# Windowed layer's channel products on quarters of TensorE, stores from ScalarE's queue, and a new order of steps in an eight-part decoder kernel

## The chip, the cores and the metric

The kernel runs on one core of one Trainium2 chip. The metric is device microseconds of one execution. The kernel before takes 1657.0 us (median of 3 runs, 1656.43 to 1660.24).

## The reference

A residual stream `x` of 16 x 64 rows of 512 floats passes four pairs of attention and feed-forward, each added to the stream after a layer norm, all in fp32 but where bf16 is named:

```python
x = x + L0_xattn(norm(x), ctx)   # windowed attention over 16 positions, 64 channels, 8 heads
x = x + L0_ffn(norm(x))          # int8-quantised gate/up/down
x = x + L1_xattn(norm(x), ctx)   # 32 query heads, 8 key heads of 128, q and k RMS-normed
x = x + L1_ffn(norm(x))          # block-scaled 4-bit weights and activations (bf16 products)
x = x + L2_xattn(norm(x), ctx)   # 32 heads of 16
x = x + L2_ffn(norm(x))          # router, 16 of 64 low-rank experts
x = x + L3_xattn(norm(x), ctx)   # 16 query heads, 4 key heads of 96
x = x + L3_ffn(norm(x))          # 3-bit weights, dequantised

def L0_xattn(x, cond, Wq, bq, Wk, bk, Wv, bv, Wo, bo):   # x as (16, 64 channels, 512)
    q, k, v = (W @ src + b for ...)                      # W is 64 x 64, over the channels
    dots = sum over a head's 8 channels of q[t] * k[t + w], w in 16 window places
    out = softmax(dots * 8 ** -0.5) applied to v[t + w]
    return Wo @ out + bo
```

## The kernel before

The stream lies in SBUF as 8 tiles of 128 rows (two of the 64-row sequences each). Two lanes of work are written into one program and one instruction order. The **main** lane (lane `a`, four PSUM banks) does `normed_attention` (the second layer's attention) on all tiles, then the rest of the layers on tiles 4 to 7. The **side** lane (lane `b`, four other banks) does the first layers (`WindowAttention`, then `Int8Ffn`) for groups of two tiles, then the later layers on tiles 0 to 3. `merged` runs the main generator and, after each step, advances the side generator by as much estimated cost as the main step yielded, times a rate. A `Need` makes the main lane stop until the side lane has reached a mark, so that a group's first layers are in the stream before the main lane reads it; meanwhile only side work is written. TensorE's order is that of the writing. The other engines' orders are made by a scheduler; `behind_main` puts an instruction behind the main lane's latest VectorE instruction.

`normed_attention` has two loops over `ticks`, which runs every step of a unit with a lag in ticks. The first, the **context stage**, has 32 units: keys and values of the context (`ps_ckv`, L757), a copy `ckv` (L766), squares (L768), a factor `r` by GpSimd's power (L123), scaled keys turned by TensorE (`ps_ckT`) and written back (L782), and a store `saved` to DRAM (L784) from SyncE's queue. The buffer of `ckv` is used again six units on. The second, the **main loop**, has 64 units; a tick writes `scores`, `scale`, `queries` (`ps_q`), `project` (`ps_wo`, added to the stream by VectorE at L157), `turn` (`ps_qT`, `ps_kT`), `keys_values` (`ps_kv`), `turn_weights` (`ps_pT`), `values` (`ps_a`), in this order. Each of the eight takes a PSUM bank, and four banks go round, so each result waits for the reader of the fourth before it.

`WindowAttention` multiplies two sequences of 64 channels at a time with a block-diagonal 128 x 128 weight `wbd`: for each tile three products to `qs`, `kp`, `vp` (`inputs`, L323) and one, in two halves of the columns, for the output (`project`, L461). `dots` are products on VectorE summed over channels by TensorE on 32-column tiles of the array (L364). They go through DRAM to another layout (`dots_d`, L374 and L376), through a softmax on VectorE, ScalarE and GpSimd (`softmax`), through DRAM again (`att_d`, L400), and are loaded spread over 8 channels each (`att`, L412; four buffers). `output` then forms products (L438) and sums (L448, GpSimd) over 8 window groups. The first group yields an extra pause of 16 before `output`, and 4 after it.

All DMAs stand in SyncE's queue. Some waits there are for a buffer to come free and some for an earlier transfer on the same completion counter.

`small_head_attention` holds products on tiles of the array of 32 rows by 64 columns (L1101). `mxfp4_ffn` takes ticks of quantise 8.0, product 0.9, turn 0.3.

Of the kernel before, what the change touches and what calls it, by code (L numbers as in the profile page):

```python
# [8 lines left out]
F32 = mybir.dt.float32  # L9
# [219 lines left out]
class WindowAttention:  # L229
# [4 lines left out]

    WIN, LEFT, NH = 16, 8, 16
# [4 lines left out]
    def __init__(self, es, ln, ctx_in, wt, bias):  # L240
        self.ln, self.ctx_in = ln, ctx_in
        k, nc = ln.k, ln.nc
        NH = self.NH
        pool = ln.pool(es, "l0c", 1)

        self.group = pool.tile([P, 2, 2 * NH], F32, tag="group", name="group")
        nc.gpsimd.memset(self.group, 0.0)
        for j in range(2):
            nc.vector.tensor_reduce(
                self.group[:, j, NH * j : NH * (j + 1)],  # L250
                k.ident.rearrange("p (h d) -> p h d", d=8),
                AX.X,
                ALU.add,
            )
        self.dram = es.enter_context(
            ln.tc.tile_pool(name="turned", bufs=2, space=bass.MemoryType.DRAM)
        )

        self.wbd = pool.tile([P, 4, P], F32, tag="wbd", name="wbd")
        nc.gpsimd.memset(self.wbd, 0.0)  # L260
        self.bcol = pool.tile([P, 4], F32, tag="bcol", name="bcol")
        for r in range(2):
            rows = slice(r * S, (r + 1) * S)
            nc.sync.dma_start(self.wbd[rows, :, rows], wt)
        nc.sync.dma_start(self.bcol, bias)

    def run(self, tiles, pause=0.0):

        self.pause = pause
        with ExitStack() as es:  # L270
            self.pool = self.ln.pool(es, "l0a", 1)
            cns = [self.context(t) for t in tiles]
            yield 0.0
            xns = [self.normed(t) for t in tiles]
            yield 5.0
            kept = []
            for xn, cn in zip(xns, cns):
                kept.append(self.inputs(xn, cn))
                yield 3.0
            scores = []  # L280
            for qs, kp, _ in kept:
                dots = yield from self.dots(qs, kp)
                scores.append(dots)
            weights = []
            self.loads = []
            for n, dots in enumerate(scores):
                kept_weights = yield from self.softmax(dots)
                weights.append(kept_weights)
                if n == 0:
                    self.source = weights  # L290
                    for _ in range(3):
                        self.load()
            yield 2.0 + self.pause
            rest = None
            for i, t in enumerate(tiles):
                rest = yield from self.output(i, t, kept[i][2], rest)
            yield 4.0 + self.pause / 4
            rest()
# [11 lines left out]
    def inputs(self, xn, cn):  # L310

        ln, nc, pool, LEFT = self.ln, self.ln.nc, self.pool, self.LEFT
        qs = pool.tile([P, D], F32, tag="qs", name="qs", bufs=2)
        kp = pool.tile([P, D + self.WIN], F32, tag="kp", name="kp", bufs=2)
        vp = pool.tile([P, D + self.WIN], F32, tag="vp", name="vp", bufs=2)
        for pad in (kp, vp):
            nc.gpsimd.memset(pad[:, :LEFT], 0.0)
            nc.gpsimd.memset(pad[:, LEFT + D :], 0.0)
        for j, (src, dst) in enumerate(
            ((xn, qs), (cn, kp[:, LEFT : LEFT + D]), (cn, vp[:, LEFT : LEFT + D]))  # L320
        ):
            ps = ln.bank([P, D], "ps_qkv")
            nc.tensor.matmul(ps, lhsT=self.wbd[:, j, :], rhs=src, start=True, stop=True)  # L323
            nc.scalar.activation(dst, ps, AF.Identity, bias=self.bcol[:, j : j + 1])
        return qs, kp, vp
# [5 lines left out]
    def dots(self, qs, kp):  # L331
# [23 lines left out]
        for n, (b, j) in enumerate(steps):  # L355
            prods = ahead
            if n + 1 < len(steps):
                ahead = products(*steps[n + 1])
            if n == 0:
                yield 1.0  # L360
            if j == 0:
                ps = ln.bank([P, D], "ps_dot")
            for w in range(NB // 2):
                nc.tensor.matmul(  # L364
                    ps[32 * w : 32 * (w + 1)],
                    lhsT=self.group[:, j, :],
                    rhs=prods[w // 2][:, w % 2, :],
                    start=j == 0,
                    stop=j == 1,
                )  # L370
            yield 2.5 if n else 1.5
            if j == 1:
                nc.scalar.copy(dots[:, b, :], ps)
                nc.sync.dma_start(dram[b], dots[:, b, :])  # L374
# [6 lines left out]
    def softmax(self, e):  # L381


        ln, nc = self.ln, self.ln.nc
        WIN, NPC, L = self.WIN, self.NPC, self.L
        n_at_once = L // 2
        for c in range(2):
            part = e[:, :, c * n_at_once : (c + 1) * n_at_once]
            by_place = part.rearrange("p w n -> p n w")
            mx = ln.small.tile([P, n_at_once], F32, tag="mx0", name="mx0")  # L390
            nc.vector.tensor_reduce(mx, by_place, AX.X, ALU.max)
            nc.vector.tensor_tensor(part, part, bc(mx, 1, WIN), ALU.subtract)
            nc.scalar.activation(part, part, AF.Exp, scale=8.0**-0.5)
            sm = ln.small.tile([P, n_at_once], F32, tag="sm0", name="sm0")
            nc.vector.tensor_reduce(sm, by_place, AX.X, ALU.add)
            nc.vector.reciprocal(sm, sm)
            nc.gpsimd.tensor_tensor(part, part, bc(sm, 1, WIN), ALU.mult)
            yield 3.0
        dram = self.dram.tile([WIN // 2, self.NH, 2 * D], F32, tag="att", name="att_d")
        nc.sync.dma_start(  # L400
            dram.rearrange("g h (q m) -> (h q) g m", q=NPC),
            e.rearrange("p (g w) n -> p g (w n)", w=2),
        )
        return dram
# [12 lines left out]
    def output(self, i, t, vp, rest):  # L417

# [13 lines left out]
        for g in range(n_groups):  # L432
# [22 lines left out]
            if g == 3 and rest is not None:  # L455
                rest()

        def project():
            po = ln.bank([P, D], "ps_o")
            for w in range(2):  # L460
                nc.tensor.matmul(  # L461
                    po.rearrange("p (a q n) -> p a q n", a=2, n=L),
                    lhsT=self.wbd[:, 3, :],
                    rhs=acc[:, :, :, w, :],
                    start=w == 0,
                    stop=w == 1,
                )
            x = ln.k.x[t]
            nc.vector.scalar_tensor_tensor(x, po, self.bcol[:, 3:4], x, ALU.add, ALU.add)

        return project
# [204 lines left out]
def normed_attention(ln, groups, rates, w_in, w_kv, norms):  # L676
# [7 lines left out]
    with ExitStack() as es:  # L684
# [59 lines left out]
        def factors(r, sq):  # L744

            nc.vector.tensor_reduce(r, sq, AX.X, ALU.add)
            nc.vector.tensor_scalar(r, r, 1.0 / HD, 1e-6, ALU.mult, ALU.add)  # L747
            ln.rsqrt(r, r)

        def context_keys(u):  # L750
# [18 lines left out]
            r = ln.small.tile([P, 5], F32, tag="r", name="r")[:, 0:2]  # L769
            factors(r, sq)  # L770
# [8 lines left out]
        def context_turn(u):  # L779
# [4 lines left out]
            nc.sync.dma_start(saved[u], both)  # L784
# [33 lines left out]
        def keys_values(u):  # L818
# [19 lines left out]
            factors(r, sq)  # L838
# [39 lines left out]
        def project(u):  # L878
# [9 lines left out]
            [(4, context_turn, 0.3), (2, context_scale, 0.0), (0, context_keys, 3.4)],  # L888
# [6 lines left out]
                (1, scale, 0.0),  # L895
                (0, queries, 3.4),
                (5, project, 3.4),
                (1, turn, 0.7),
                (0, keys_values, 1.7),
                (3, turn_weights, 0.4),  # L900
                (4, values, 0.9),
# [5 lines left out]
def mxfp4_ffn(ln, tiles, w_in, bias, kept_w):  # L907
# [10 lines left out]
    with ExitStack() as es:  # L918
# [76 lines left out]
        yield from ticks(units, [(0, quantise, 8.0), (2, product, 0.9), (1, turn, 0.3)])  # L995
# [181 lines left out]
def lora_experts(ln, tiles, w_a, w_r, w_b):  # L1177
# [13 lines left out]
    with ExitStack() as es:  # L1191
        pool = ln.pool(es, "l2f")
        wr = pool.tile([P, NC, KE], F32, tag="wr", name="wr", bufs=1)
        nc.sync.dma_start(wr.rearrange("p c n -> p (c n)"), w_r)
# [359 lines left out]
def decoder_kernel(ctx: ExitStack, tc: tile.TileContext, i: dict, out: bass.AP):  # L1554
# [8 lines left out]

    def first_layers(ln):
        with ExitStack() as es:
# [13 lines left out]
            first = attention.run(groups[0], 16.0)  # L1579
# [9 lines left out]
            for _ in range(6):  # L1589
                yield next(first)  # L1590
            yield MARK
            ffn.load()
            for t in range(2, NT):
                load(t)
            for n, tiles in enumerate(groups):
                yield from first if n == 0 else attention.run(tiles)
                yield from ffn.run(tiles)
                yield MARK

    def last_layers(ln, tiles):  # L1600
        yield from small_head_attention(ln, tiles, i["l2a_w"])
        yield from lora_experts(ln, tiles, i["l2f_a"], i["l2f_r"], i["l2f_b"])
# [4 lines left out]
    def side():  # L1607
        yield from first_layers(b)
        b.pages(ctx)
        yield from mxfp4_ffn(b, halves[0], i["l1f_w"], i["l1f_b"], kept_w)  # L1610
# [20 lines left out]
def laid_out(a):  # L1631
# [10 lines left out]
    i["l0a_w"] = np.stack([a[f"L0_xattn_W{n}"].T for n in "qkvo"], 1)  # L1642
# [72 lines left out]
```

## Time and profile before

The profiled execution took 1651.44 us, its span from first to last instruction 1649.7 us at a granted clock of 0.995; the runs' median is 1657.0 us.

| engine | busy us | share of the span | instructions |
|---|---|---|---|
| TensorE (PE) | 1596.5 | 97% | 7020 |
| its weight loads (PEld) | 929.2 | 56% | 7024 |
| VectorE (DVE) | 962.3 | 58% | 1998 |
| ScalarE (ACT) | 619.3 | 38% | 1929 |
| GpSimd (POOL) | 508.2 | 31% | 524 |

By stage, in us of busy time:

| stage, us from the start | length | PE | DVE | ACT | POOL | granted clock |
|---|---|---|---|---|---|---|
| start, 0 to 17 | 17 | 10.71 | 9.60 | 5.72 | 2.72 | 1.00 |
| context, 17 to 158 | 141 | 139.83 | 99.88 | 48.21 | 71.96 | 1.00 |
| hand-over, 158 to 182 | 24 | 12.39 | 12.54 | 3.75 | 8.00 | 0.77 |
| main loop with side work, 182 to 1115 | 933 | 913.93 | 610.77 | 386.57 | 345.64 | 0.99 to 1.00 |
| later layers, 1115 to 1650 | 535 | 519.66 | 229.51 | 175.03 | 79.90 | 1.00 |

An fp32 product is recorded as two passes of the array, so counts of matmuls are twice those of the code; transposes are one pass. A pass is recorded longer than the distance to the next, since passes overlap: busy time is not work done at the array's peak.

### The profile page before, as it was taken

Reading aid. Unit: us, or ns where it says so; the run is one execution under the profiler, and the core shown is the slowest. Engines: PE = TensorE matmul, PEld = TensorE weight load, DVE = VectorE, ACT = ScalarE, POOL = GpSimd, SP = SyncE. Lnnn points to the kernel's source line nnn. Section 1 sums busy time; section 2 is a strip of 40 time slices with the busy share of each in tenths; the row PEclk is TensorE's granted clock in tenths of the full one; section 3 lists DMA queues with packets and bytes.
Section 4 is the critical chain, followed back from the end, with each engine's and each line's share of the span. In section 5 each row is a group of like instructions: output and inputs, shape, how many; then the busy total and the mean of one; then the engine's idle time right before and its main releaser. Section 6 shows DMA issues by size and latency. Waiting matters only on the chain.

```text
span 1649.7 us, 20730 instructions
## 1 busy us (share of the span) xinstructions
PE 1596.5 (97%) x7020; PEld 929.2 (56%) x7024; DVE 962.3 (58%) x1998; ACT 619.3 (38%) x1929; POOL 508.2 (31%) x524
## 2 busy tenths in 40 slices
PE   8999799999999999999999999999999999999999
PEld 2334356664566645666565565554566566456774
DVE  6596498757776576766964465337345343422335
ACT  3333354344433344334343354221235432223442
POOL 1294237632484214843221232101012110011112
PEclk9999899999999999999999999999999999999999
DMA  8893159524882337934532321122120101201120
GB/s 272 248 290 113 44 155 281 169 87 139 235 257 77 129 120 211 252 133 150 183 128 96 122 80 69 54 109 85 59 71 20 48 20 51 90 16 58 39 71 26
DMA packets 98872, 200.32 MB, mean 121 GB/s; under 512 B 49488, under 2 KB 66768, under 8 KB 86992
## 3 DMA queue, kind: packets, MB, share of 16 engines
q1 hardware_dynamic: 98768, 199.00, 38.8%
q8 instruction: 57, 0.93, 0.2%
q14 instruction: 47, 0.39, 0.1%
HBM read 179.57 MB, written 19.40 MB: 121 GB/s over the span
## 4 chain that ended last, share of the span: by engine, by line
PE 87%; DVE 5%; DMA 3%; ACT 2%; POOL 1%; issue 1%; SPq 0%; ACTq 0%; POOLq 0%; DVEq 0%
PE ps_wo L670 16%; PE ps_q L805 11%; PE ps_ckv L757 6%; PE ps_kv L823 6%; PE ps_q L1411 5%; PE ps_s L620 5%; PE ps_a L661 5%; PE ps_o L1262 3%; PE ps_pT L141 3%; PE ps_h L1237 3%; PE ps_v L1358 3%; PE ps_k L1395 3%; PE ps_dot L364 2%; PE ps_q L1083 2%; PE ps_wo L1151 2%; PE ps_o L1324 2%
## 5 line engine op out<-in xcount | busy, mean ns | idle before, releaser
L670 PE MATMUL ps_wo<-l1a_o,aT 128*128 128x512 f32 x512 | 231.5, 595 | 2.0 <-ACT aT L875 2.0
L805 PE MATMUL ps_q<-l1a_w,kvT 128*128 128x512 f32 x512 | 231.8, 596 | 0.0
L645 POOL TENSOR_TENSOR p<-p,sm 128x512 f32<-128x512 f32 x96 | 103.1, 1074 | 362.2 <-DVE sm L644 328.3
L636 ACT ACTIVATE p<-ps_s,mx 128x128 f32<-128x128 f32 x384 | 135.6, 370 | 162.0 <-DVE mx L631 143.5
L123 POOL TENSOR_TENSOR r<-r,mhalf 128x5 f32<-128x5 f32 (+1 forms) x96 | 101.0, 1052 | 304.5 <-DVE r L747 284.7
L157 DVE TENSOR_TENSOR x<-x,ps_wo 128x512 f32<-128x512 f32 x104 | 71.2, 685 | 199.3 <-PE ps_wo L670 171.6
L670 PEld LDWEIGHTS ps_wo<-l1a_o,aT 128*128 128x128 f32 x512 | 95.4, 190 | 118.4 <-issue 111.1
L805 PEld LDWEIGHTS ps_q<-l1a_w,kvT 128*128 128x128 f32 x512 | 93.3, 192 | 95.9 <-issue 95.8
L448 POOL TENSOR_TENSOR acc<-acc,pv 128x512 f32<-128x512 f32 x96 | 126.3, 1339 | 7.5 <-DVE pv L438 6.4
L823 PE MATMUL ps_kv<-l1a_w,kvT 128*128 128x256 f32 x512 | 121.4, 380 | 0.6 <-ACT qn L815 0.6
L757 PE MATMUL ps_ckv<-l1a_kv,kvT 128*64 128x512 f32 x512 | 116.9, 598 | 0.5 <-ACT ckv L766 0.5
L823 PEld LDWEIGHTS ps_kv<-l1a_w,kvT 128*128 128x128 f32 x512 | 92.6, 190 | 14.3 <-issue 1.9
L123 POOL TENSOR_TENSOR rs<-rs,mhalf 128x1 f32<-128x1 f32 x64 | 36.8, 580 | 206.7 <-DVE rs L132 195.0
L620 PEld LDWEIGHTS ps_s<-kT,qT 128*128 128x128 f32 (+1 forms) x704 | 89.8, 193 | 6.2 <-issue 2.1
L620 PE MATMUL ps_s<-kT,qT 128*128 128x128 f32 (+1 forms) x704 | 91.9, 276 | 0.0
L343 DVE TENSOR_TENSOR prod<-qs,kp 128x1024 f32<-128x1024 f32 x64 | 77.5, 1248 | 14.5 <-PE ps_dot L364 7.6
L670 PE MATMUL ps_wo<-l3a_o,aP 128*128 128x512 f32 x192 | 85.6, 593 | 0.0
L1411 PE MATMUL ps_q<-kvT,l3a_w 128*128 128x256 f32 x384 | 85.5, 379 | 0.0
L652 DVE COPY pT<-ps_pT 128x512 f32<-128x512 f32 x96 | 64.2, 682 | 35.1 <-PE ps_pT L141 35.1
L438 DVE TENSOR_TENSOR pv<-att,ps_v 128x512 f32<-128x512 f32 x128 | 81.0, 676 | 3.5 <-DMA att<-att_d 3.3
L853 ACT COPY qT<-ps_qT 128x512 f32<-128x512 f32 x64 | 37.5, 587 | 120.7 <-PE ps_qT L141 120.7
L141 PE MATMUL ps_pT<-ident,p 128*128 128x128 f32 x512 | 72.8, 274 | 8.1 <-DVE x L157 8.1
(194 smaller groups left out, 2725.8 us busy)
## 6 DMA issues: line engine op xcount, KB each, us to landing
l1a_w<-in_l1a_w SPq DMA_DIRECT2D x32, 1536.0 KB, 6.9
att<-att_d SPq DMA_DIRECT2D x64, 512.0 KB, 7.8
l1a_o<-in_l1a_w SPq DMA_DIRECT2D x32, 1024.0 KB, 5.1
s<-ckv SPq DMA_DIRECT2D x32, 256.0 KB, 5.9
l3a_w<-in_l3a_w SPq DMA_DIRECT2D x6, 1024.0 KB, 5.5
l3a_o<-in_l3a_w SPq DMA_DIRECT2D x8, 768.0 KB, 4.1
l1a_kv<-in_l1a_kv SPq DMA_DIRECT2D x4, 1024.0 KB, 7.9
dots_d<-dots SPq DMA_DIRECT2D x16, 256.0 KB, 2.9
```

Source lines behind the costliest of these rows:

```text
L123: self.nc.gpsimd.tensor_tensor(out, v, self.k.mhalf[:, : v.shape[1]], ALU.pow)
L141: self.nc.tensor.transpose(ps[:, c, :], src[:, c * P : (c + 1) * P], ident)
L448: nc.gpsimd.tensor_tensor(sums, before, pv, ALU.add)
L620: nc.tensor.matmul(ps[:, i, :], lhsT=qT[:, i // 2, 2 * (i % 2) : 2 * (i % 2) + 2, :].rearrange("p g s -> p (g s)"), rhs=kTs[i // 2], start ...
L636: nc.scalar.activation(p[:, i, :], ps[:, i, :], AF.Exp, bias=mx[:, i : i + 1], scale=self.scale, accum_out=sm[:, i : i + 1],)
L645: nc.gpsimd.tensor_tensor(p, p, bc(sm, 2, P), ALU.mult)
L661: self.nc.tensor.matmul(ps[:, j, :, :], lhsT=v[:, j, :], rhs=pT[:, j, :], start=True, stop=True)
L670: self.nc.tensor.matmul(ps, lhsT=a, rhs=wo[:, g, :], start=g == 0, stop=g == len(chunks) - 1)
L757: nc.tensor.matmul(ps[j * S : (j + 1) * S], lhsT=k.context(c, 2 * t + 1 - j), rhs=w_pair[hp][:, c, :], start=c == 0, stop=c == NC - 1,)
L805: nc.tensor.matmul(ps, lhsT=k.stream(c, t), rhs=w_qkv[n][0][:, c, :], start=c == 0, stop=c == NC - 1,)
L823: nc.tensor.matmul(ps, lhsT=k.stream(c, t), rhs=w_qkv[n][1][:, c, :], start=c == 0, stop=c == NC - 1,)
L1411: nc.tensor.matmul(ps[:, j], lhsT=wq[:, c, (j0 + j) * P : (j0 + j + 1) * P], rhs=k.kvT[:, c, t : t + 2, 1:3, :], start=c == 0, stop=c == N ...
```

## The change

- `wbd` (block-diagonal) becomes `w4`, one DMA of a weight laid out in all four 64 x 64 quarters. `at_once` does a pair of products as four matmuls of 64 rows by 64 columns, one on each quarter. `inputs` becomes `keys_values` for each tile and one `queries` for both; `project` does both tiles of a group after the second `output`, where the first tile's stood within the second's.
- In the first group, `dots_d` and `att_d` are stored from ScalarE's queue; in all groups `saved` is. The int8 weights are asked for behind the first group's dots and tiles 2 to 7 of `x` behind its attention, as the program writes it; the pause of 16 becomes 2. In the other groups the softmax's VectorE steps stand behind the main lane's.
- Context stage: the factors of two units are computed together, and scaling and turning lag 3 and 5 ticks (2 and 4 before).
- Main loop: `project` stands ahead of `queries`, `values` ahead of `turn_weights`.
- `mxfp4_ffn`: quantise 6.5 and turn 1.8 of the tick's 9.2. The router's weights of `lora_experts` are loaded once for both lanes.

```diff
-        for r in range(2):
-            rows = slice(r * S, (r + 1) * S)
-            nc.sync.dma_start(self.wbd[rows, :, rows], wt)
+        nc.sync.dma_start(self.w4, wt)
...
+        self.pause, self.first = pause, late is not None
+        self.queue = self.ln.nc.scalar if self.first else self.ln.nc.sync
...
-            for xn, cn in zip(xns, cns):
-                kept.append(self.inputs(xn, cn))
-                yield 3.0
+            for n, cn in enumerate(cns):
+                keys.append(self.keys_values(n, cn))
+                yield 1.5
+            queries = self.queries(xns)
+            yield 3.0
...
+            if late is not None:
+                late()
...
+    def at_once(self, *products, start=True, stop=True):
+        for r in range(2):
+            rows = slice(r * S, (r + 1) * S)
+            for ps, j, src, swapped in products:
+                out = slice((r ^ swapped) * S, ((r ^ swapped) + 1) * S)
+                self.ln.nc.tensor.matmul(
+                    ps[out], lhsT=self.w4[rows, j, out], rhs=src[rows], start=start, stop=stop
+                )
+    def keys_values(self, n, cn):
...
+        pss = [ln.bank([P, D], "ps_kv0") for _ in range(2)]
+        self.at_once((pss[0], 1, cn, n), (pss[1], 2, cn, 1 - n))
...
+    def queries(self, xns):
...
+        self.at_once(*[(ps, 0, xn, n) for n, (ps, xn) in enumerate(zip(pss, xns))])
...
-                nc.sync.dma_start(dram[b], dots[:, b, :])
+                self.queue.dma_start(dram[b], dots[:, b, :])
...
-            nc.vector.tensor_reduce(mx, by_place, AX.X, ALU.max)
-            nc.vector.tensor_tensor(part, part, bc(mx, 1, WIN), ALU.subtract)
+            with ExitStack() if self.first else ln.behind_main():
+                nc.vector.tensor_reduce(mx, by_place, AX.X, ALU.max)
+                nc.vector.tensor_tensor(part, part, bc(mx, 1, WIN), ALU.subtract)
...
-            if g == 3 and rest is not None:
-                rest()
...
+    def project(self, tiles, accs):
...
+        for w in range(2):
+            self.at_once(
+                *[
+                    (po, 3, acc[:, :, :, w, :], 1 - n)
+                    for n, (po, acc) in enumerate(zip(pos, accs))
+                ],
+                start=w == 0,
+                stop=w == 1,
+            )
...
+            if n % 2 == 0:
+                fresh.append(ln.small.tile([P, 5], F32, tag="r", name="r"))
+            r = fresh[-1][:, 2 * (n % 2) : 2 * (n % 2) + 2]
+            nc.vector.tensor_reduce(r, sq, AX.X, ALU.add)
+            if n % 2:
+                factors(fresh[-1][:, 0:4])
...
-            nc.sync.dma_start(saved[u], both)
+            nc.scalar.dma_start(saved[u], both)
...
-            [(4, context_turn, 0.3), (2, context_scale, 0.0), (0, context_keys, 3.4)],
+            [(5, context_turn, 0.3), (3, context_scale, 0.0), (0, context_keys, 3.4)],
...
+                (5, project, 3.4),
                 (0, queries, 3.4),
-                (5, project, 3.4),
                 (1, turn, 0.7),
                 (0, keys_values, 1.7),
+                (4, values, 0.9),
                 (3, turn_weights, 0.4),
-                (4, values, 0.9),
...
-        yield from ticks(units, [(0, quantise, 8.0), (2, product, 0.9), (1, turn, 0.3)])
+        yield from ticks(units, [(0, quantise, 6.5), (2, product, 0.9), (1, turn, 1.8)])
...
-            first = attention.run(groups[0], 16.0)
+            first = attention.run(groups[0], 2.0, ffn.load)
```

## The prediction

> **What bounds the kernel.** I read the page's first part, the groups by shape on PE, PE's waits, and the timelines of the places they name.
>
> ```profile
> PE 1596.5 (97%) x7020; PEld 929.2 (56%) x7024; DVE 962.3 (58%) x1998; ACT 619.3 (38%) x1929; POOL 508.2 (31%) x524
> ```
>
> No other engine passes 58%, so what counts is PE's work and PE's waits. The groups by shape (busy, mean of one | idle before) give the work:
>
> ```profile
> L323 PE MATMUL ps_qkv<-cn,wbd 128*128 128x512 f32 x32 | 16.3, 634 | 0.0
> ...
> L461 PE MATMUL ps_o<-acc,wbd 128*128 128x512 f32 x32 | 15.2, 599 | 0.0
> ...
> L757 PE MATMUL ps_ckv<-l1a_kv,kvT 128*64 128x512 f32 x512 | 116.9, 598 | 0.5 <-ACT ckv L766 0.5
> ...
> L1101 PE MATMUL ps_s<-kbd,qT 32*64 32x128 f32 x512 | 10.4, 279 | 0.8 <-DVE x L157 0.8
> ```
>
> Busy over count is what a pass costs among its neighbours. A full-array pass costs 0.475 us at L461, a half-array one (128*64) 0.228 at L757: two share the array. At L1101 it is 10.4/512 = 0.020 for 128 columns, where a full pass of 128 columns costs about 0.11 (below): most of eight small tiles run together.
>
> PE's timeline (start, length, idle before) gives the step without overlap:
>
> ```profile
> 508.71 3.60 PE L670 MATMUL ps_wo<-l1a_o,aT 128*128 128x512 f32 x8
> 512.15 0.60 PE L141 MATMUL ps_qT<-ident,qn 128*128 128x128 f32 x4
> 512.58 0.27 PE L141 MATMUL ps_kT<-ident,kn 128*128 128x128 f32 x1
> ```
>
> Eight passes take 512.15 - 508.71 = 3.44, 0.43 each; a transpose (512.58 - 512.15)/4 = 0.11.
>
> PE's waits (total, times, longest):
>
> ```profile
> PE ps_pT L141 <- DVE x L157: 8.1, 4, 3.2
> ...
> PE ps_o L989 <- ACT xT L979: 3.6, 5, 0.8
> ...
> PE ps_wo L670 <- ACT aT L875: 2.0, 3, 0.7
> ...
> PE ps_a L661 <- DVE x L157: 1.8, 2, 1.1
> ```
>
> The other large ones lie in the hand-over, where the side lane alone is written. PE's timeline there:
>
> ```profile
> 159.94 0.41 PE L141 MATMUL ps_ckT<-ident,ckn 128*128 128x128 f32 x2 [1.50 <-DVE ckn L776]
> ...
> 165.07 1.98 PE L583 MATMUL ps_dn<-w_l0f,qT 128*128 128x512 f32 x4 [1.05 <-POOL qT L534]
> 170.23 0.44 PE L141 MATMUL ps_q<-ident,xs 128*128 128x128 f32 x2 [3.17 <-DVE xs L526]
> 171.98 3.78 PE L583 MATMUL ps_dn<-w_l0f,qT 128*128 128x512 f32 x4 [1.31 <-POOL qT L534]
> 175.56 1.06 PE L141 MATMUL ps_xT<-ident,xn 128*128 128x128 f32 x4
> 181.20 1.11 PE L141 MATMUL ps_xT<-ident,xn 128*128 128x128 f32 x4 [4.59 <-DVE rs L132]
> 182.11 4.91 PE L805 MATMUL ps_q<-l1a_w,kvT 128*128 128x512 f32 x8
> ```
>
> Last, VectorE's timeline at the longest L157 wait:
>
> ```profile
> 634.97 1.98 DVE L391 TENSOR_REDUCE mx<-dots 128x32 f32<-128x512 f32 x2 [4.52 <-DMA dots<-dots_d]
> ...
> 639.18 0.68 DVE L157 TENSOR_TENSOR x<-x,ps_wo 128x512 f32<-128x512 f32 x1
> ```
>
> VectorE stood at the side lane's softmax, waiting for a DMA, and the main lane's add stood behind it with a PSUM bank.
>
> **Quarter products.** A group has 2 x 3 + 2 x 2 = 10 full products, 20 passes, 8.6 us. After, it has 20 products of half the size on each side, in five sets of four, 40 passes. With all four quarters at once a set costs two steps, 0.86, a group 4.3. The trace shows no 64*64 tile. Bounds: no overlap, 40 x 0.43 = 17.2; full overlap, 4.3. I take 4.3, as L1101 is the nearest row. Entering and leaving a tiled shape costs: a context tick (64.65 to 68.60 in the timeline, 3.95) holds 16 half passes (3.44) and two transposes (0.22), so 0.3. Three visits a group: 0.9. Saved per group: 8.6 - 4.3 - 0.9 = 3.4; for groups 1 to 3, where PE is full, 10.2 us.
>
> In the first group the three products stand at the start, where the end is set elsewhere: `prod` began at 10.90 after `kp` and now waits for `qs`, ScalarE's fifth 0.69 us step. Context rows land about 1 us earlier (one issue fewer, smaller queue ahead), PE begins near 5.6 on the half clock (0.85 a pass), has three sets done at 10.5, ScalarE reaches `qs` at 11.4. So first `ps_ckv` at 17.1 against 16.57: +0.5. The first group's output saves 1.7 - 0.3 = 1.4.
>
> A rule that speaks against this part is the Trainium skill's "TensorEngine Tiling (Array Packing)", Restrictions and Gotchas: different row tiles cannot access one PSUM bank at the same time. At L1101 the row groups write different banks, so this trace does not test it; both halves of a product here do share a bank, on different partitions. By the rule the sum loses the rival's 17 us; I keep it as that rival.
>
> **Hand-over.** The pause falls by 14 + 3.5 and the first dots no longer queue behind SyncE's loads (the second half's copy ended at 22.8, its store was issued at 32.9). In the new order both `ps_o` follow the 24th context unit (21st and 25th before) and the first `ps_gu` the 26th, so the int8 layer runs among context units. Before, the idle from 17 to 182 is 12.8 us (0.7 near 76, the rest above), and passes on the slow clock add about 2.2. After remain: from the last `ps_dn` to `ps_q`, the add and norm chain (0.75 + 1.27 + 0.69 + 0.33 + 0.56 + 0.55, with hops 4.8) less ten turns and four transposes (1.5) = 3.3; and twice about 1.2 where `ps_gu` directly follows its transposes (copy 0.69, clip 0.61). Sum: -15.0 + 5.7 = -9.3. It needs the sums `acc` ready when PE reaches `ps_o`, near 114 us; before, they were ready at 130.4. The first attention tile, at 68.4 before, should land near 50.
>
> **Stores on ScalarE.** 38 issues of about 0.38 us (SyncE's `saved` rows) join a context tick of 0.59 + 0.48 + 0.42: 1.9 of 3.95, so no cost while none waits. Queued behind a waiting store are the `ckv` copies that free PE's banks; PE can run two units ahead. The store of unit n must land before the copy of n + 6: about 6.5 us after its issue. Bounds: 0, and the third rival's.
>
> **Main loop.** From `ps_wo` to the next use of its bank lay turn and `ps_kv` (0.44 + 0.11 + 1.72 = 2.3); now lie `ps_q` and turn (4.0). So 1.7 more for each of six waits on L157 (8.1 + 1.8 = 9.9), and the softmax behind the main lane takes away the cause of the two like the one shown: about 0.9 stays, -9.0. In return `ps_q`'s bank is wanted by `ps_a` 2.3 us later instead of by `ps_kv` 4.0 later. In the trace the copy `qn` (L815) would exceed this in 8 of 64 ticks, 5.0 us in all; ScalarE is freer of `p` by then, so I take 4. `ps_wo` follows `ps_a` by 1.3 (transposes, scores); `aT` is ready 1.0 us after the start of the last `ps_a` pass in the median, 1.33 at most, so nothing there. Net -5.0, between -9 and 0. At the loop's end the three waits of `ps_wo` on `aT` get 0.4 between: -1.2.
>
> **The rest.** The first tile of a group joins the output late: its norm, 2 us, is now on the way to `ps_q`, whose distance is 10.7 to 11.3 us of PE work against a chain of 8 to 10.5; +1.5 over groups 1 to 3. `mxfp4_ffn`'s order now has main work ahead of two of five waits on `xT`: -1.3. Four instead of two VectorE reductions for `group`, the factors in pairs (16 GpSimd steps of 0.7 fewer), one router load, the moved int8 and `x` loads (almost the same places in SyncE's order): 0, covered by PE's work; a few tenths if not.
>
> Sum: +0.5 - 1.4 - 9.3 - 10.2 - 5.0 - 1.2 + 1.5 - 1.3 = -26.4. The profiled execution took 1651.4, so 1625.0; the runs' median lies 5.6 above it, so 1631.
>
> **Rivals.**
> 1. The two row halves of a product take turns: each of 20 sets costs 1.72, +17: 1648. For: no row shows a bank shared so. Against: the halves write different partitions, and L757 shows two writers of one bank side by side. 0.08.
> 2. The hand-over stays: the window sums are late at `ps_o` or the int8 chain at its transposes, and PE waits inside the context stage instead: +9.3, 1640. For: the page's 58 us of GpSimd in 76 to 158 leave little room. Against: the earlier start and fewer power steps. 0.15.
> 3. Slower: ScalarE's stores wait for transfers on their completion counter, and the `ckv` copies with them. A tick has 3.95 - 1.9 = 2.1 of room; from a wait of 2.9 per store (26.4/32 more) the gain is gone; at 3.5, 32 x 1.4 = 45 us: 1676. For: before, ScalarE did once stand for a store's landing,
>
> ```profile
> 75.75 0.59 ACT L766 COPY ckv<-ps_ckv 128x512 f32<-128x512 f32 x1 [6.57 <-DMA s<-ckv]
> ```
>
> and PE lost 0.7. Against: the waits in the new order name transfers issued a tick or more before. 0.06.
> 4. The gains cancel against small waits: 1657. 0.03.
>
> **Numbers.** The forecast has 0.68. A measurement tells 0.3%, 5 us, from no change. Faster: the forecast, the second rival and most of the first, 0.90; same 0.04; slower 0.06. The range 1616 to 1649 takes in the first two rivals and a main loop without its 4 us for `qn` and a hand-over with no idle, with the runs' spread of 3.8.
>
> **What the profile would show.** Passes of 64*64 at about 0.11 busy each (0.22 for the first rival); `ps_q` first near 172; no wait on L157 over 1.5 us and some on L815; ScalarE's copies in the context stage waiting for PE, not DMA. I am wrong if the first main-loop `ps_q` comes after 180, if the 64*64 group costs over 30 us, or if waits on `qn` exceed what L157 gave.

## The result, and the profile after

The changed kernel took 1649.8 us (median of 11 runs, 1644.8 to 1653.8) against 1657.0 before (11 runs): a ratio of 0.9949, 95% interval 0.9934 to 0.9964. A second set of runs gave 0.9961 (0.9944 to 0.9978). So it is faster by 6 to 7 us, where 26 were forecast; the sign is right and the size is not. The profiled execution took 1650.1 us, only 1.3 below the one before. That one was lower than all of its kernel's other runs (1651.4 against a median of 1657.0); this one lies on its median.

The page's first part:

```profile
PE 1592.2 (97%) x7104; PEld 918.8 (56%) x7104; DVE 963.0 (58%) x1984; ACT 615.6 (37%) x1929; POOL 498.7 (30%) x507
```

TensorE still sets the time. PE's waits (total, times, longest) answer to those of before:

```profile
PE ps_ckv L802 <- ACT ckv L811: 7.3, 5, 2.3
PE ps_gu L597 <- POOL qT L578: 5.4, 4, 2.1
PE ps_wo L714 <- ACT aT L926: 3.1, 3, 2.2
PE ps_o L326 <- POOL acc L481: 2.5, 2, 2.2
...
PE ps_kv L873 <- DVE x L157: 1.9, 5, 0.7
...
PE ps_a L705 <- ACT qn L865: 0.6, 1, 0.6
```

The last two lines are as forecast or better: the waits on the add L157 fell from 9.9 to 1.9, none over 0.7, and the copy `qn` (L815 before, L865 now) costs 0.6. The first line is new (0.5 before): TensorE waits for the copies `ckv`, which stand in ScalarE's queue. PE's timeline at the end of the hand-over:

```profile
183.40 0.41 PE L141 MATMUL ps_ckT<-ident,ckn 128*128 128x128 f32 x2 [1.00 <-DVE ckn L826]
...
186.17 1.11 PE L141 MATMUL ps_xT<-ident,xn 128*128 128x128 f32 x4 [1.00 <-DVE xn L134]
187.08 1.91 PE L855 MATMUL ps_q<-l1a_w,kvT 128*128 128x512 f32 x2
```

The large waits of before (3.2 and 4.6) are gone from here, yet the main loop's first `ps_q` stands at 187.1, not near 172 and not even at the 182.1 of before. The quarter products in PE's timeline (start, length):

```profile
506.99 1.95 PE L326 MATMUL ps_o<-acc,w 64*64 64x512 f32 x16
508.86 1.13 PE L705 MATMUL ps_a<-pT,v 128*128 128x256 f32 x4
...
584.97 1.09 PE L326 MATMUL ps_kv<-cn,w 64*64 64x512 f32 x8
585.99 0.66 PE L141 MATMUL ps_pT<-ident,p 128*128 128x128 f32 x4
```

Sixteen quarter passes take 508.86 - 506.99 = 1.87, or 0.117 each, and eight take 1.02. In the records of the first visit they start four at a time, the four within 0.02 us, the next four 0.41 to 0.46 later: the four quarters run together.

To see where time is lost, PE's program can be laid end to end at the prediction's prices (0.43 for a full pass, other shapes in proportion, a 64*64 pass a quarter). That gives about 1551.7 us before and 1534.6 after: at these prices the quarters save 17.2 over four groups. What a trace takes beyond that is loss: waits, half-clock time, changes of shape. The table gives it by the place in PE's program, counted in us of such work from the main loop's first `ps_q`; the last column adds up. It ends at PE's last pass, some 4 us before the end of the span. "Again" is a second execution of the changed kernel; the others follow below.

| kernel | first `ps_q` at | loss up to it | 0 to 50 | 50 to 150 | 150 to 500 | 500 to 750 | rest | all |
|---|---|---|---|---|---|---|---|---|
| before | 182.1 | 36.5 | 3.4 | 0.4 | 16.0 | 6.2 | 31.4 | 93.9 |
| changed | 187.1 | 45.8 | 6.9 | 5.4 | 18.0 | 8.3 | 25.4 | 109.8 |
| changed, again | 179.7 | 38.4 | 6.8 | 12.4 | 17.1 | 8.3 | 25.4 | 108.4 |
| stores by SyncE | 176.9 | 35.6 | 4.8 | 11.3 | 23.9 | 8.2 | 25.4 | 109.2 |
| that, softmax as before | 179.3 | 38.0 | 6.1 | 3.0 | 20.1 | 8.0 | 25.4 | 100.6 |

The change gained 17.2 us of work and about 6 in the rest; it lost 2 to 9 ahead of the main loop and 13 to 19 in the 750 us of work behind. Two executions of one program differ by 7.4 in their first `ps_q`, and the earlier one loses 7.0 more between 50 and 150. It is not the early start that costs this: laid out the same way, the three other traces below with the softmax held lose 11.5 to 12.7 there, and their loops start at 183.1 to 186.3. The first trace's 5.4 is the exception.

Recorded waits are the smaller part of what the loop lost. In the 750 us, PE's recorded idle time is 14.5 us before and 15.7 in the first trace after, and half-clock time costs 3.0 and 4.3. The rest, about 9.6 before and 19.0 after, lies in steps from pass to pass that are longer than their price with no wait recorded. About 3.6 of the 9.4 more stand at the quarter products (entries, and a late sum `acc` in group 1), about 1.5 at the sums of the dots, and the remainder in small pieces all over the loop. Every trace of the experiments below has 17 to 21 there.

### The profile page after: what moved, and what is told of

The parts are those of the page before. It is cut to its first block, busy times and chain, and to the rows that moved or that the text cites. A ratio compares the mean times of both kernels' runs of the same rounds, so it can differ in the third digit from the quotient of the medians.

```text
span 1648.3 us, 20789 instructions
## 1 busy us (share of the span) xinstructions
PE 1592.2 (97%) x7104; PEld 918.8 (56%) x7104; DVE 963.0 (58%) x1984; ACT 615.6 (37%) x1929; POOL 498.7 (30%) x507
## 4 chain that ended last, share of the span: by engine, by line
PE 75%; DVE 11%; DMA 5%; issue 4%; ACT 3%; POOL 2%; SPq 0%; ACTq 0%; POOLq 0%; DVEq 0%
PE ps_wo L714 15%; PE ps_q L855 10%; PE ps_kv L873 5%; PE ps_q L1461 5%; PE ps_s L664 4%; PE ps_a L705 4%; PE ps_o L1312 3%; PE ps_h L1287 3%; PE ps_pT L141 3%; PE ps_ckv L802 3%; PE ps_v L1408 3%; PE ps_k L1445 2%; PE ps_wo L1202 2%; PE ps_q L1134 2%; PE ps_o L1374 2%
## 5 line engine op out<-in xcount | busy, mean ns | idle before, releaser
L123 POOL TENSOR_TENSOR r<-r,mhalf 128x5 f32<-128x5 f32 (+1 forms) x80 | 95.1, 1188 | 281.2 <-DVE r L792 269.8
L157 DVE TENSOR_TENSOR x<-x,ps_wo 128x512 f32<-128x512 f32 x104 | 70.6, 679 | 115.1 <-PE ps_wo L714 82.8
L481 POOL TENSOR_TENSOR acc<-acc,pv 128x512 f32<-128x512 f32 x96 | 122.6, 1305 | 5.9 <-DVE pv L471 4.8
L888 DVE TENSOR_REDUCE r<-sq 128x5 f32<-128x640 f32 x64 | 52.2, 816 | 102.6 <-ACT sq L881 102.4
L863 ACT ACTIVATE sq<-ps_q 128x512 f32<-128x512 f32 x64 | 38.2, 598 | 155.0 <-PE ps_q L855 155.0
L471 DVE TENSOR_TENSOR pv<-att,ps_v 128x512 f32<-128x512 f32 x128 | 82.0, 676 | 21.0 <-DMA att<-att_d 18.1
L374 DVE TENSOR_TENSOR prod<-qs,kp 128x1024 f32<-128x1024 f32 x64 | 78.9, 1272 | 14.5 <-ACT qs L355 7.0
L664 PEld LDWEIGHTS ps_s<-kT,qT 128*128 128x128 f32 (+1 forms) x704 | 85.0, 192 | 3.4 <-issue 2.1
```

Of the source, the lines that this page charges most:

```text
L123: self.nc.gpsimd.tensor_tensor(out, v, self.k.mhalf[:, : v.shape[1]], ALU.pow)
L374: nc.vector.tensor_tensor(prod, bc(qs, 1, 2), spaced(kp, b * NB + j + 2 * w, [[2, 2], [1, D]]), ALU.mult,)
L471: nc.vector.tensor_tensor(pv.rearrange("p (q w n) -> p q w n", w=2, n=L), att[:, a, :].rearrange("p (q w n) -> p q w n", w=2, n=L), spaced ...
L481: nc.gpsimd.tensor_tensor(sums, before, pv, ALU.add)
L664: nc.tensor.matmul(ps[:, i, :], lhsT=qT[:, i // 2, 2 * (i % 2) : 2 * (i % 2) + 2, :].rearrange("p g s -> p (g s)"), rhs=kTs[i // 2], start ...
```

## The experiments

**The `saved` stores back on SyncE's queue.**

```diff
-            nc.scalar.dma_start(saved[u], both)
+            nc.sync.dma_start(saved[u], both)
```

Why this was tried is in ScalarE's timeline of the changed kernel (start, length, idle before and what ended it):

```profile
55.05 0.59 ACT L811 COPY ckv<-ps_ckv 128x512 f32<-128x512 f32 x1 [6.58 <-DMA s<-ckv]
...
60.35 0.63 ACT L425 ACTIVATE dots<-dots 128x512 f32<-128x512 f32 x1 [4.04 <-DVE dots L424]
60.89 0.57 ACT L811 COPY ckv<-ps_ckv 128x512 f32<-128x512 f32 x1
...
67.28 0.38 ACTq L434 DMA_DIRECT2D att_d<-dots  x1
67.76 0.59 ACT L811 COPY ckv<-ps_ckv 128x512 f32<-128x512 f32 x1 [4.46 <-POOL dots L431]
...
74.11 0.59 ACT L811 COPY ckv<-ps_ckv 128x512 f32<-128x512 f32 x1 [5.09 <-DMA s<-ckv]
```

Four copies in a row are late, for three reasons: a store that has not landed (twice), an exponential that waits for its gathered scores, and the `att_d` store that waits for GpSimd and keeps ScalarE from the copy behind it. They cost PE 0.9, 2.3, 1.8 and 1.2; a fifth copy, at 110.85, waits for a landing again (1.1). The store issued at 63.33 landed at 74.03. It had to land within about 6.5 us by the prediction.

The DMA share of 40 to 76 us is 0.98, against 0.79 before, but this average alone does not set the landing. Time to landing of the stores `s` issued between 65 and 70 us in the kernel before (four; the two issued ten us earlier took 3.5), and between 45 and 64 in the changed one (four) and in the one below with all stores on SyncE's queue (six; its share is 0.98 too):

```profile
DMA to landing us min/median/max: 9.2/10.1/11.2
...
DMA to landing us min/median/max: 8.0/8.7/10.7
...
DMA to landing us min/median/max: 4.6/5.5/7.0
```

> The changed kernel with the `saved` stores alone given back to SyncE's queue; the first group's stores stay on ScalarE's. Theory (ScalarE's stores hold the `ckv` copies and these hold PE): the waits of `ps_ckv` on the copy L811 fall from 7.3 us to below 2, the first `ps_q` of the main loop moves from 187.1 to about 178, and the time falls by 7 to 10, to about 1641. Rival 1 (the copy waits for the landing of a buffer's last store, whichever queue issued it, because the DMA engines are full between 40 and 76 us): waits stay at 5 to 8 us, first `ps_q` between 185 and 189, time within 3 us of the changed kernel's 1650. Rival 2 (SyncE's queue becomes long and holds the attention tiles): `ps_o` waits for `acc` by more than its 2.2 us and the time is 1652 to 1656.

Measured: 1649.1 (0.9959, 0.9944 to 0.9975), waits on L811 3.0, first `ps_q` at 183.1. The waits fell by more than half, and those that stayed stand where the exponential and the `att_d` store do. The time did not move, as the first rival had it. The theory's size fell.

**All stores on SyncE's queue.**

```diff
-        self.queue = self.ln.nc.scalar if self.first else self.ln.nc.sync
+        self.queue = self.ln.nc.sync        # and the edit above
```

> The changed kernel with all stores on SyncE's queue, the first group's `dots_d` and `att_d` too. Theory: the copies no longer stand behind the store that waits for GpSimd's weights (67.28, PE lost 1.2) either; waits on L811 below 1 us, first `ps_q` about 176, time 1 to 2 us below the run with the `saved` stores alone moved. Rival 1 (full DMA engines): like the changed kernel, 1647 to 1653. Rival 2 (SyncE's queue): attention tiles land later, `ps_o` waits for `acc` by 5 us or more, time 1652 to 1658.

Measured: 1647.2 (0.9959, 0.9943 to 0.9975), no wait on L811 at all, first `ps_q` at 176.9. The theory was right: the place is 10 us earlier than in the first trace, and the time 1.9 below the run before by the medians, though by the ratios the two are equal. Little of the 10 us reached the end. Where it went is seen in VectorE's timeline of this run:

```profile
295.49 0.68 DVE L696 COPY pT<-ps_pT 128x512 f32<-128x512 f32 x1
300.55 0.69 DVE L471 TENSOR_TENSOR pv<-att,ps_v 128x512 f32<-128x512 f32 x1 [4.38 <-DMA att<-att_d]
301.15 0.68 DVE L674 TENSOR_REDUCE mx<-ps_s 128x4 f32<-128x512 f32 x1
301.87 0.80 DVE L675 TENSOR_SCALAR mx<-mx 128x4 f32<-128x4 f32 x1
302.58 0.68 DVE L897 TENSOR_TENSOR qn<-qn,r 128x512 f32<-128x512 f32 x1
```

and in PE's:

```profile
297.83 3.60 PE L855 MATMUL ps_q<-l1a_w,kvT 128*128 128x512 f32 x8
303.40 0.63 PE L141 MATMUL ps_qT<-ident,qn 128*128 128x128 f32 x4 [1.98 <-DVE qn L897]
```

A product of the side lane waited 4.38 us for its attention tile, with the main lane's `mx` and `qn` behind it in VectorE's order, and TensorE stood for `qn`. The windows after it (length, then busy time of PE, PEld, DVE, ACT and POOL, granted clock, DMA share, GB/s):

```profile
300.00:304.00 4.00, 2.02 (x8) 0.77 (x6) 2.87 (x5) 1.22 (x7) 1.26 (x1) 1.00 0.91 293
304.00:311.00 7.00, 6.28 (x19) 1.50 (x19) 1.50 (x4) 2.00 (x6) 2.30 (x2) 0.51 0.02 4
```

For 7 us (two windows of 3.41) the clock was halved, which costs 3.4 us more than the waits themselves.

**The first stage as before.** Stores by SyncE, pause 16, int8 weights and `x` loaded ahead, lags 4 and 2, factors one by one; all else as changed.

```diff
-            [(5, context_turn, 0.3), (3, context_scale, 0.0), (0, context_keys, 3.4)],
+            [(4, context_turn, 0.3), (2, context_scale, 0.0), (0, context_keys, 3.4)],
-            first = attention.run(groups[0], 2.0, ffn.load)
+            first = attention.run(groups[0], 16.0, lambda: None)    # ffn.load(), load(t) after MARK
```

> The changed kernel with its whole first stage as in the kernel before (stores by SyncE, pause 16, int8 weights and x loaded ahead, distances 4 and 2, factors one unit at a time); quarter products, loop order and all the rest stay changed. Theory (the first stage lost what the rest gained): first `ps_q` at 180 to 182, so 5 to 7 us below the changed kernel, about 1644. Rival (the loss sits behind the first stage, in clock steps and changes of tile shape): first `ps_q` at 180 to 182 all the same, but the end within 2 us of the changed kernel's 1650, or above it.

Measured: 1653.6 (0.9990, 0.9977 to 1.0002), first `ps_q` at 185.1. The theory fails; of the rival the end holds ("or above it"), its first `ps_q` does not. The old stage is worse here. Against the changed kernel the new stage is worth 4 us by the medians, and 5 or 7 by the ratios (0.9961 and 0.9949, its two sets); it is not the loss I took it for.

**The main loop's order as before.**

```diff
-                (5, project, 3.4),
                 (0, queries, 3.4),
+                (5, project, 3.4),
                 (1, turn, 0.7),
                 (0, keys_values, 1.7),
-                (4, values, 0.9),
                 (3, turn_weights, 0.4),
+                (4, values, 0.9),
```

> The changed kernel with the main loop's steps in the order of the kernel before. The prediction's term (order worth 5.0, loop end 1.2): 1656, waits on the add L157 back at 8 to 10 us. Rival (what the order saves in L157 it gives back in waits on GpSimd, `aT` and `sc` and in slow-clock passes): time within 2 us of 1650 although the L157 waits come back.

Measured: 1652.6 (0.9988, 0.9975 to 1.0000). Waits on L157 came back at 7.2 before `ps_pT`, `ps_s` and `ps_a`, and those of `ps_wo` on `aT` fell from 3.1 to 1.4. The order is worth 3 us by the medians, and 4.5 or 6.5 by the ratios beside the changed kernel's two sets: from between the two expectations up to the prediction's 6.2.

**The changed kernel once more, and the softmax as before.**

```diff
-            with ExitStack() if self.first else ln.behind_main():
+            with ExitStack():                   # twice; one yield of 3.0 for two of 1.5
```

> The changed kernel once more, unaltered, beside the others of this call. Theory (its waits are those of its order, and what scatters is which of them are followed by a half-clock window of 3.41 us): the waits of `ps_ckv` on the copy L811 again 6 to 9 us, the first `ps_q` at 186 to 188, the time within 2 us of 1650. Rival (the first trace was an unlucky one): first `ps_q` before 180.

> The changed kernel with the attention softmax as before (not held behind the main lane's VectorE work, one pause of 3 after it). Theory (held softmax starts the attention loads 6 us later against the main loop, where the DMA engines are full, so VectorE waits 15 to 20 us for attention tiles instead of 3.3 and holds the main lane's steps): VectorE's waits for `att` fall to below 8 us, the waits of PE on `qn` and `acc` in the loop fall by 2 to 3, time 1645 to 1648. Rival (the prediction's: the softmax ahead of the main lane costs L157 waits): waits on L157 of over 1.5 us come back at a softmax, time 1650 to 1654.

The changed kernel again took 1649.7, with waits of 5.4 on L811 (6 to 9 expected), and its first `ps_q` came at 179.7: the time is as the theory had it, the place as the rival had it, and the first trace had been a late one. With the softmax as before: 1646.9 (0.9941, 0.9922 to 0.9960), as that theory had it. VectorE's waits for `att` fell from 18.1 in the first trace to 4.5, PE's on `qn` from 1.5 to 0.5, but not those on `acc` (2.5 and 2.8). PE's waits on L157 before `ps_kv` stayed at 1.6, none over 0.7. So the new order of the loop keeps these away by itself.

**Both undone: stores by SyncE, softmax as before.**

> All stores on SyncE's queue and the softmax as before. Theory: both losses are undone; first `ps_q` at 177 and no PE wait of 2 us near 303, so 3 to 6 us below the run with the stores alone moved, 1641 to 1644. Rival (what the early hand-over gains the DMA-bound group 1 takes back in any order): a wait of 2 us or more on `qn`, `acc` or L157 between 295 and 315 again, time 1646 to 1649.

Measured: 1642.5 (0.9925, 0.9904 to 0.9946), as the theory had it, with the first `ps_q` at 179.3 instead of 177 and no PE wait of 2 us near 303. By its median this was the best of the kernels that do the whole computation, 13 us below the kernel before in its set of runs and 7 below the changed one run beside it; the intervals of these two just touch. The four combinations make a square, in us below the kernel before of the same set: 6.0 (both changes), 8.4 (stores undone), 8.9 (hold undone), 13.2 (both undone). A single step of 2 to 3 us in it lies within the intervals. VectorE's waits in this run:

```profile
DVE pv L470 <- DMA att<-att_d: 4.8, 4, 1.8
```

with 15.7 in the run with the stores alone moved and 3.3 before. The first attention load of group 1 is issued 60.7 us after the first `ps_q` before, 67.9 and 67.8 in the changed kernel, 61.1 here. Over the twelve traces with all loads, those below among them, these waits divide by the hold: 14.9 to 20.8 us in the six with it, 3.3 to 7.5 in the six without it. The hold makes the loads 5 to 7 us late against the loop, into a stretch where the DMA share is 1.0 for about 50 us.

**Half of the attention loads left out.** Stores by SyncE, softmax held. In groups 1 to 3 every second tile `att` is not loaded and the one before it used again; this kernel and the last one below leave out that part of the computation.

```diff
+            if not self.first and n % 2:
+                self.loads.append(self.loads[-1])
+                return
             att = self.pair("att")
```

> All stores on SyncE's queue; in groups 1 to 3 every second attention tile is not loaded and the one before it is used again, which leaves 4 MB per group out of the transfers and changes the result. Theory (transfers bound group 1's attention): the DMA share between 250 and 290 falls well below 1, VectorE's waits for `att` vanish, no PE wait of 2 us on `qn` near 303, time 5 to 9 us below the run with the stores alone moved, 1638 to 1642. Rival (GpSimd's sums `acc` and VectorE's order bound it): VectorE waits for `acc` instead, the waits of PE stay, time 1645 to 1648.

Measured: 1642.2 (0.9916, 0.9900 to 0.9932), at the edge of the theory's range and 5.0 below the run with the stores alone moved, and the two intervals do not meet. The DMA share fell from 1.0 to 0.40 between 280 and 290, the waits for `att` to 4.9, the loss of 50 to 150 from 11.3 to 5.2. So the transfers bind there.

**More pause, and room for `aT`.** Both start from the best kernel.

```diff
-            first = attention.run(groups[0], 2.0, ffn.load)
+            first = attention.run(groups[0], 8.0, ffn.load)
```

> All stores on SyncE's queue, softmax as before, and a pause of 8 in place of 2 ahead of the first group's output. Theory (the window sums, ready near 120 us, are late for `ps_o`, as the second rival had it): `ps_o`'s wait of 2.7 us on `acc` in the context stage goes, with the half-clock window it can bring, and the first `ps_q` comes 2 to 4 us earlier, near 176; time 2 to 3 us below the 1642.5 of the pause of 2. Rival (the int8 chain behind it sets the end of the stage): the wait goes, but waits of `ps_gu`, `ps_ckT` and `ps_xT` after 140 us grow by as much, first `ps_q` at 179 or later, time 1642 to 1645.

```diff
+                (4, values, 0.9),
                 (0, keys_values, 1.7),
-                (4, values, 0.9),
```

> All stores on SyncE's queue, softmax as before, and in the main loop `values` one step ahead of `keys_values`, so that 3.0 us of PE work instead of 1.3 lie between the last `ps_a` and `ps_wo`. Theory (the new order left `aT` too little room: two 0.63-us exponentials of the softmax in ScalarE's queue make PE wait 1.9 us, and a half-clock window costs 1.7 more): the waits of `ps_wo` on `aT` in the main loop go, time 2 to 4 us below 1642.5. Rival (the room is taken from another step): PE waits for `pT`, or `ps_a` for L157, by 3 us or more in all, time 1642 to 1646.

> Both edits together. If each is worth what its theory says, 4 to 7 us below 1642.5, near 1637; if both rivals hold, 1642 to 1647.

Measured: 1647.1 (0.9954, 0.9936 to 0.9971), 1644.7 (0.9938, 0.9922 to 0.9954) and 1646.9 (0.9944, 0.9927 to 0.9960). The 1642.5 is of another set of runs, and its interval overlaps all three. The rivals held in what they say of the waits; the pause's time is 2 above even its rival's. With the longer pause the wait of 2.7 on `acc` went, and PE's timeline shows what took its place:

```profile
171.39 3.22 PE L626 MATMUL ps_dn<-w_l0f,qT 128*128 128x512 f32 x4 [2.12 <-POOL qT L577]
174.40 1.06 PE L141 MATMUL ps_xT<-ident,xn 128*128 128x128 f32 x4
180.04 1.11 PE L141 MATMUL ps_xT<-ident,xn 128*128 128x128 f32 x4 [4.58 <-DVE rs L132]
```

That is the hand-over of before, back again: a few us later in PE's order, and the int8 chain has no context unit left to run beside. With `values` moved, the waits on `aT` fell from 3.5 to 0.9 and two others rose (PE's waits):

```profile
PE ps_a L704 <- DVE x L157: 3.9, 4, 1.4
PE ps_kv L872 <- ACT qn L864: 3.8, 3, 3.3
```

**Half of the loads left out, softmax as before.**

> All stores on SyncE's queue, softmax as before, and every second attention tile of groups 1 to 3 left out (the one before it is used again, the result changes). Theory (the held softmax cost time only because it made the attention loads late in full queues, so taking the hold away and halving the loads cure the same loss): within 2.5 us of the run without the hold, 1640 to 1643. Rival (two separate losses, the hold in VectorE's order and the transfers): the gains add, 1636 to 1638, as each was worth about 5.

Measured: 1638.4 (0.9895, 0.9878 to 0.9911, four runs), between the two. In these two traces the loss of 50 to 150 is 3.0 with all loads and 3.0 with half of them: there the two are one cause. The hold is not the only cause of loss in that stretch, though: the three kernels with more pause or more room, which have no hold, lose 7.9 to 9.8. The first `ps_q` is 2.0 earlier, ahead of any load that this edit touches, and differs by more between two executions of one program. What the rest of the medians' 4 us is stays open.

## Why the prediction was wrong

**Hand-over (-9.3, start +0.5): failed, the largest miss.** The bound that I had set for being wrong, a first `ps_q` after 180, was passed in the first trace (187.1), not in the second (179.7); the forecast was 172. The start took more: TensorE waits for the context rows until 7.4, not 5.6, and the first `ps_ckv` is at 18.9, not 17.1. Then I left 5.7 us of idle to `ps_q`; the first trace has 14.9, and 8.5 us at half clock, which cost another 4.2. Together these make about the 15 us from 172 to 187. Seven of the idle time are late copies `ckv` in ScalarE's queue: 4.3 on three copies whose store had not landed, and 3.0 on two that stood behind an exponential and behind the `att_d` store. That is near the third rival, which I gave 0.06, but neither its mechanism (a store that waits on its completion counter) nor its price per store. The step that failed is in "Stores on ScalarE", where a store that "must land before the copy of n + 6: about 6.5 us after its issue" was put at nothing: four stores issued between 45 and 64 us took 8.0 to 10.7. The trace before had four that took 9.2 to 11.2 (the one shown with the third rival is among them), so it spoke against that bound already. Why the landing times differ so is open. And I did not ask what else of the first group would now stand in that queue. Another 2.2 are the second rival's: the sums `acc` were late at `ps_o`. With all stores on SyncE's queue the waits on the copies went and `ps_q` came at 176.9, still not 172. By the experiment with the old stage, the whole new stage gained 4 to 7 us all the same.

**Main loop order (-5.0) and loop end (-1.2): right mechanism, half to all of the size.** L157 fell as said (9.9 to 1.9). The waits on L815 that I took 4 for are only 0.6. But that `aT` is ready at most 1.33 after the last `ps_a` pass starts, "so nothing there", was read from a trace in which no exponential of the softmax stood in front of that copy; it cost 2.2 at 647. By the experiment the order is worth 3 to 6.5.

**What I priced at a gain: the softmax behind the main lane.** I counted it with the L157 waits and did not ask what its later end delays. Its output feeds 16 loads of 0.5 MB per group, in a stretch with the DMA share already at 1.0 (visible in the windows of before, 250 to 300 us). By the medians the hold costs about 3 with the stores as changed and about 5 with them on SyncE; the intervals of the first pair overlap and those of the second just touch, so the sign rests on both pairs and on the waits for `att`. The gain that I had counted for it was not there to be had: without the hold the waits on L157 stayed low. Five of the six traces with the hold lose 11.3 to 12.7 between 50 and 150, wherever their loop starts; the two with no other change to the steps lose 3.0 (stores on SyncE) and 6.7.

**Quarter products (-10.2): right by the visits.** Summed over their visits, groups 2 and 3 take 4.78 and 4.94 where 8.58 stood, and the pass before a visit costs 0.1 more, so 3.3 to 3.5 a group for the forecast's 3.4. Group 1 takes 6.1, as its output waited for `acc` in the middle. No run puts the full products back, so what the quarters bring to the whole time was not measured. The first rival is refuted: 0.117 a pass, not 0.22. The Trainium skill's "TensorEngine Tiling (Array Packing)", Restrictions and Gotchas, forbids two row tiles one bank at a time; here both halves of a product write one bank on different partitions and do not take turns.

**`mxfp4` (-1.3), FFN norm (+1.5).** The waits of `ps_o` on `xT` went from 3.6 to 1.7 and one of 0.7 on `mv` came: -1.2. The other was not measured by itself. The rest of the program lost 6 us less than before (31.4 to 25.4), more than I had for it.

**The offset.** I added 5.6 for the distance of the profiled execution from the median; the changed kernel's profiled execution has none. By profiles the miss is 25, by medians 19. The parts do not add up to the result: -10 (quarters by their visits, groups 1 to 3), -4 to -7 (stage) and -3 to -6.5 (order) make -17 to -23, the hold takes 3 back, and 6 to 13 us are not assigned to a part. The table shows them as loss in the loop; by PE's records most of that loss is in longer steps without a recorded wait, alike in all the kernels with quarter products. Its cause stays open.

## What to carry to other kernels

A queue that also holds work which frees the bottleneck's buffers should get only transfers whose inputs are ready and whose landing nothing behind them needs soon; take the landing times from the slowest stretch of the trace, not from its median. An instruction put behind others to keep them free is late for its own readers; follow its output to the transfers that it starts. And an earlier hand-over need not reach the end: here 10 us at the first `ps_q` were 3 us or less in the time.

## What the runs showed of the hardware

In these traces the granted clock is full or half, and each stretch between two changes is a whole number of windows of 3.41 us. I cut the 14 traces of this case into these windows, from the first record of the clock on (10 to 13 us into each, so the 1.00 of the start before says nothing of its first passes). Of windows at full clock with 2.0 us or more of PE idle, 48 of 48 were followed by one at half clock; of those with 0.7 to 1.2 us, 0 of 166; between 1.2 and 2.0, 31 of 99. So a wait of 2 us costs 1.7 more (half of 3.41) if it falls into one window, and can cost nothing more if it is split: the wait of 3.2 us at 640 in the trace before was split 1.9 and 1.3 and stayed free. This may be one source of the spread between executions, which was not tried by itself; it makes waits of 2 us (of 1.8 us or more there were six in the trace before and eight in the one after, that of the first matmul left out) worth more than their length. The Trainium skill's "TensorE: Matmul & The Clock Gate", What's actually happening, gives a free-running window of 3413 ns, which the traces agree with; its advice (Why this matters for your kernels) to avoid idle of over some 3 us between bursts is too lenient here, where 2.0 in one window was enough.
